# Moving half of an image's column layout from the prologue into layer 0, and reordering the passage to layer 1

## The chip, the cores and the metric

The kernel runs on one core of a Trainium2 chip. The metric is the device time of one execution in microseconds (us). Most executions of a kernel agree within 0.3%. The engines are PE (TensorE: matmuls and transposes), DVE (VectorE), ACT (ScalarE), POOL (GpSimd) and SP (SyncE, which issues most of the DMAs here). PE writes to PSUM, the others compute from SBUF or PSUM; 16 DMA engines move data between SBUF and the device's memory.

## The reference

The input x has shape (4, 16, 256, 256), float32: 4 images of 16 channels. Two layers follow, each with a residual:

```python
x = x + _L0_conv_ref(_gn(x), conv_w, conv_b)
x = x + _L1_conv_ref(_gn(x), base_weight, spline_weight, spline_scaler, bias_weight)
```

`_gn` normalises groups of two channels over the whole image (8 groups). Layer 0 is a 3x3 convolution from 16 to 400 channels, read as 25 logits for each of 16 channels at each pixel. A softmax over the 25 gives weights, and the output is the weighted sum of the pixel's 5x5 neighbourhood in the same channel:

```python
out = conv(x, conv_w, padding='SAME') + conv_b
weights = softmax(out.reshape(N, C, 25, H, W), axis=2)
return einsum('ncuij,ncuij->ncij', unfold5x5(x), weights)
```

Layer 1 takes each normalised pixel through SiLU and through 8 cubic B-spline basis functions; both sets of features go through a 3x3 convolution to 16 channels, and a bias is added.

## The kernel before, in words

**Layouts.** An image is handled in two halves `h` of 128 rows (rows are SBUF partitions), and a half in 8 strips of 32 columns: 64 strips in all, image by image, upper half first. Layer 0 reads three copies of the normalised image in device memory: `hs`, rows for the 5x5 neighbourhoods; `hst[b][h]`, the columns (transposed, 130 rows each: a half and one border row above and below); and `hsl[b][h]`, the same columns split into a rounded part `hi` and the remainder `lo`. `normalize(b, ...)` (line 264) makes these copies. It is a generator: each `next` does one step. For each quarter `q` of the channels, `rows(q)` has ACT normalise the x tile twice (lines 327 and 340: into the row layout `hsp`, and into `ht`). For `n` in 0, 1 and each half, `columns(q, n, h)` has PE transpose four pieces of `ht` into the PSUM tile `tp` (line 362), copies them to `tts[n]` and, rounded, `his[n]` (lines 355 to 359; the 128x4 copies are the border row that the other half needs), and subtracts on DVE to get `los[n]` (line 370). A list `moves` holds issues that fall due some steps later: row stores (line 288) after 4 steps, loads of the next x tile (line 280) after 4, ACT copies of the border into `los` (lines 312 and 313) after 5, and six column stores of 260 KB (line 302: three tiles, two halves) after 9. All these DMAs go to SP's queue.

**Prologue** (lines 399 to 589). It loads all four images for the statistics of the first normalisation (line 423 issues a load, DVE line 536, ACT's square line 543, PE line 546), prepares weights, and in between, with two steps per group of channels, runs `normalize(0, ...)` from tiles `held`. A check of the largest possible logit sets `flag`, which each engine reads at the branch (line 1110).

**Layer 0** (`layer0`, line 622). For each strip, 8 groups of 4 columns: PE makes the logits (lines 832 and 836) from the tiles `am` and `an` (lines 648 and 658, loaded two tiles of 8 columns ahead, 3 buffers), ACT takes the exponential (line 855) into `e` (4 buffers), POOL multiplies it by the neighbourhoods `u` (line 860; `u` loaded in line 672), and DVE reduces both over the 25 taps into `nd` (line 700), one group late. Each group ends with one `next` of the preparation of the following image, which so takes most of the 16 strips of an image; the last strip of an image finishes it. Some groups later the quotient of a strip is formed (DVE lines 720 to 722) and POOL subtracts it from `xc` (line 728). After four strips `xc` (1 MB) is stored to `x1s` (line 781), and its statistics for the second normalisation are taken. For the last strip these are DVE and POOL instructions (lines 759 to 773), and its store is issued by POOL. A written order (`in_order`, line 592) fixes the order on each engine as the program emits it.

**The passage and layer 1** (`layer1`, line 888). 64 units of 16 rows follow. For each, `load_x` (line 942) loads x into one of three tiles `xta`, `xtb`, `xtc`, 8 times over the partitions, 2 MB in two DMAs; `load_tiles` (line 957) loads 0.5 MB into one of three tiles `sl`, `slb` for the SiLU. ACT forms distances (line 990), and ACT and DVE the spline (lines 158 to 169) in two parts with the temporaries `ta` and `tb`, into the ring of rows `ring`. ACT applies the SiLU in `sl` (line 972), PE runs both convolutions (lines 1036 and 1046), DVE adds the bias (line 1019). The first instructions of layer 1 are placed before the last ones of layer 0, by marks that `layer0` returns. Tiles of layer 1 lie in the memory of layer 0's pools, one pool after the other, so that a tile can be written only when the tiles under it are done with. In order and in bytes per partition, layer 0 has `prep` (58880), `im` (24960), `l0` (two `u` of 11520, four `e` of 12800), `nd` (three of 4096) and `x1` (three `xc` of 8192, `z` 1024); layer 1 has `xta` (17408), `ta` and `tb` (three of 9216 each), `xtb` (17408), `pad` (1032), `ring` (51600), `sl` (8256), `xtc` (17408), `slb` (two of 8256) and the output tiles.

Of the kernel before, what the change touches and what calls it, by code (L numbers as in the profile page):

```python
# [11 lines left out]
F32 = mybir.dt.float32  # L12
F32R = mybir.dt.float32r
AF = mybir.ActivationFunctionType
# [20 lines left out]
def conv_preact_kernel(  # L35
# [12 lines left out]
    nc = tc.nc  # L48
# [3 lines left out]
    P = 128  # L52
# [208 lines left out]
                    hsl[b][h][:, :, w : w + RP].rearrange("c t r -> (c t) r"), zero[:, 0:RP],  # L261
                )

    def normalize(b, ptr, tiles, held=None, copier=None):

        prep, xps, tts, his, los = tiles
        copier = copier or nc.scalar.copy

        moves = [(20 + 4 * i, f) for i, f in enumerate(zeros(b, nc.sync))] if held is None else []

        def move():
            for f in [f for i, f in moves if i <= 0]:
# [18 lines left out]

        def put_columns(q, n):
            g0 = n * QG
            for h in range(NH):

                for to, ti, t in ((hst, 0, tts[n]), (hsl, 0, his[n]), (hsl, 1, los[n])):
                    d = to[b][h]
                    m = 2 if to is hsl else 1  # L300
                    t = t if t.dtype == F32 else t.bitcast(F32)
                    nc.sync.dma_start(
                        bass.AP(
                            tensor=d.tensor,
                            offset=d.offset + q * QC * m * CT + ti * CT + (1 + g0) * RP,
                            ap=[[QW * RP, W // QW], [m * CT, QC], [1, QG * RP]],
                        ),
                        t[:, h].rearrange("p g r -> p (g r)"),
                    )
# [5 lines left out]
        hts = {}  # L315

        def rows(q):
            for h in range(NH):
                xp = xps[h] if held is None else held[h][:, q * QC : (q + 1) * QC]
                hsp = prep.tile([P, NST, QC, SP], F32, name=f"hsp{b}_{q}_{h}", tag="hsp")  # L320
                ht = prep.tile([P, QW, W // QW, QC], F32, name=f"ht{b}_{q}_{h}", tag=f"ht{h}")
                hts[q, h] = ht
                for k in range(QC // GC):
                    g = q * (QC // GC) + k
                    kc = slice(k * GC, (k + 1) * GC)
                    how = dict(scale=nrm[b][:, 0, g : g + 1], bias=nrm[b][:, 1, g : g + 1])
                    nc.scalar.activation(
                        hsp[:, :, kc, :].rearrange("p s c w -> p c s w"),
                        bass.AP(
                            tensor=xp.tensor, offset=xp.offset + k * GC * (W + 2 * PAD),  # L330
                            ap=[xp.ap[0], [W + 2 * PAD, GC], [SW, NST], [1, SP]],
                        ),
                        AF.Identity, **how,
                    )
                    if k == QC // GC - 1:
                        nc.scalar.copy(hsp[:, 0, :, 0:PAD], zpad)
                        nc.scalar.copy(hsp[:, NST - 1, :, PAD + SW :], zpad)
                        moves.append((4, partial(put_rows, q, h, hsp)))
                    yield
                    nc.scalar.activation(  # L340
                        ht[:, :, :, kc].rearrange("p g w c -> p c w g"),
                        xp[:, kc, PAD : PAD + W].rearrange("p c (w g) -> p c w g", g=QW),
                        AF.Identity, **how,
                    )
                    if k == QC // GC - 1:
                        moves.append((4, partial(load, q + 1, h)))
                    yield

        def columns(q, n, h):

            tp = ptr.tile([P, QG, P], F32, name=f"tp{b}_{q}_{n}_{h}", tag="tp")

            def copy(t, to):

                to(t[:, h, :, 1 : 1 + P], tp)
                if h == 0:
                    to(t[:, 1, :, 0:1], tp[:, :, P - 1 :])
                else:
                    to(t[:, 0, :, RP - 1 :], tp[:, :, 0:1])

            for k in range(QG):
                nc.tensor.transpose(
                    tp[:, k, :], hts[q, h][:, n * QG + k].rearrange("p w c -> p (w c)"), ident
                )
            yield
            copy(tts[n], copier)
            copy(his[n], nc.scalar.copy)
            yield

            nc.vector.tensor_sub(  # L370
                los[n][:, h, :, 1 : 1 + P], tp, his[n][:, h, :, 1 : 1 + P].bitcast(F32)
            )
            if h == NH - 1:
                moves.append((5, partial(border, los[n])))
                moves.append((9, partial(put_columns, q, n)))
            yield
            yield
            yield
            yield

        for h in range(NH):
            load(0, h)
        yield
        for _ in rows(0):
# [2 lines left out]
        for q in range(C // QC):  # L387
            ahead = rows(q + 1) if q + 1 < C // QC else iter(())
            for n in range(QW // QG):
                for h in range(NH):  # L390
                    for k, _ in enumerate(columns(q, n, h)):
                        if k % 3 == 2:
                            next(ahead, None)
                        move()
                        yield
            for _ in ahead:
                move()
                yield
# [5 lines left out]
    with tc.tile_pool(name="prep0", bufs=2) as prep, tc.tile_pool(  # L404
# [121 lines left out]
        for b in range(B):  # L526
# [44 lines left out]
            if b == 1:  # L571
                prepare1()
            if b == 0:
                ahead = normalize(0, ptr0, tiles, held, nc.vector.tensor_copy)
                next(ahead)
        for _ in ahead:
            pass
# [42 lines left out]
    def layer0(shift):  # L620
# [4 lines left out]
        with tc.tile_pool(name=f"prep{arm}", bufs=2) as prep, tc.tile_pool(  # L625
# [62 lines left out]
            def after(k, f, *args):  # L688

                later.append([k, partial(f, *args)])  # L690
# [34 lines left out]
            def apply(n, nd, xc):  # L725
                w0 = strips[n][2] * SW % CX
                v = xc[:, :, w0 : w0 + SW]
                nc.gpsimd.tensor_sub(v, v, nd[:, 1])  # L728
                seeds[1:] = [newest(POOLE)]
                if w0 + SW == CX:  # L730
                    if n == len(strips) - 1:
                        after(1, last_statistics, n, xc)
                    else:
                        for g in range(G):
                            after(1 + g, statistics, n, xc, g)
                    after(2, store, n, xc)

            def columns_of(n):
                b, hf, s = strips[n]
# [57 lines left out]
            for n, (b, hf, s) in enumerate(strips):  # L797
                if (hf, s) == (0, 0):
                    for _ in ahead:
                        pass  # L800
                    ahead = normalize(b + 1, ptr, tiles) if b + 1 < B else iter(())
                    if b == B - 1:
                        bank = ptr.tile([P, QG, P], F32, name=f"ps{arm}", tag="tp")
                        first_scales = [scales(k, partial(lambda k: bank[:, k], k)) for k in range(2)]
                last = (hf, s) == (NH - 1, NST - 1)
                if last:
                    for _ in ahead:
                        pass
                u = us.pop(0)
                if s * SW % CX == 0:  # L810
# [3 lines left out]
                for j in range(0, SW, JG):  # L814
# [51 lines left out]
                    if len(waiting) > LAG:  # L866
                        sums()
                    step()
                    next(ahead, None)
                    if b == B - 1 and j % (SW // 2) == 0 and s > 0:  # L870
                        next(first_scales[j // (SW // 2)], None)
                if n == len(strips) - NST // 2:
# [12 lines left out]
    def layer1(arm, last, marks, seeds):  # L885
# [5 lines left out]
        with ExitStack() as pools:  # L891
# [1 line left out]
                return pools.enter_context(tc.tile_pool(name=f"{name}{arm}", bufs=bufs, **kw))  # L893


            def temps(name):
                p = pool(name)
                return [p.tile([P, RU // 2 + 1, W], F32, name=f"{name}{k}{arm}") for k in range(3)]

            def fixed(name, shape, n=1):  # L900
                p = pool(name)
# [1 line left out]
                return t  # L903

            XT = [P, RU + 1, W]
            xt0, tmp0, tmp1 = fixed("xta", XT), temps("ta"), temps("tb")
            xt1, pad = fixed("xtb", XT), fixed("pad", [P, W + 2])[0]
            ring = fixed("ring", [P, 3 * RU + 2, W + 2])[0]
            SL = [P, RU // RT, W + 2]
            sl = fixed("sl", SL)  # L910
            xtt = xt0 + xt1 + fixed("xtc", XT)
            sl += fixed("slb", SL, 2)
            yop = pool("yo", 3)
            pstat = pool("pstat1", space=PSUM)
            py = pool("py", 4, space=PSUM)
# [144 lines left out]
            load_tiles(0)  # L1060
            for half in range(2):
                load_x(1, half)
            nc.gpsimd.tensor_copy(pad, edge[:, 4:5].to_broadcast([P, W + 2]))
            for e in (0, W + 1):
                nc.gpsimd.tensor_copy(
# [6 lines left out]

            halo(0)
            set_up = newest(POOLE).name
            sides(sl[0])
            features(0, put)
            first_silu = len(nc.cur_bb.bb.instructions)
            silu(0)
            for n in range(len(units)):
                if n % 2:  # L1080
                    next(more, None)
                if n > 0:
                    features(n, put)
                    silu(n)
                    halo(n)
                if n + 2 < len(units):
                    for half in range(2):
                        load_x(n + 2, half)
                store()
                if n + 1 < len(units):  # L1090
                    load_tiles(n + 1)
                outputs(n)
                if n == 0:
                    for t in sl[1:]:
                        sides(t)
            for _ in range(LAG1):
                put(1)
                store(1)
# [61 lines left out]
```

## Time and profile before

| | us |
|---|---|
| median of 3 runs | 3076.96 |
| lowest and highest | 3075.38, 3077.81 |
| the profiled execution's own time | 3072.98 |
| its span | 3070.8 |
| busy in the span: DVE | 2959.4 |
| PE | 2807.1 |
| ACT | 2238.8 |
| POOL | 1954.8 |

The span reaches from the first to the last instruction of the profiled execution; the execution's own time has some 2 us around it. An engine's busy time is the sum of what its instructions took, without register and DMA-issuing ones. A line such as L700 is line 700 of the kernel. In a row of a view, `out<-in` names the written and the read tiles, `x512` is the number of instructions, and what stands in brackets, or after the bar, is the idle time before them and what ended it. SPq is SP's queue, in which DMAs are issued. The DMA share is the mean busy share of 16 DMA engines; it can go a little above 1.

### The profile page before, as it was taken

To read this page: it belongs to the slowest core of one execution; us is meant where nothing else is said; L and a number is where in the kernel's file an instruction comes from. 1 tells how busy PE (TensorE), PEld (TensorE's weight loads), DVE (VectorE), ACT (ScalarE), POOL (GpSimd) and SP (SyncE) were. 2 spreads that over 40 slices of the span, in tenths; PEclk is the share of its full clock that TensorE was granted. 3 is DMA by queue.
4 is the path that set the end of the run, shared out by engine and by line. 5 is a ranking of instruction groups with operands and counts; after the bars stand their busy time and mean duration, and the time that the engine had idled before them with its cause. 6 is when DMAs were issued, how large, how long until landed. Compare 5 with 4: busy or idle time off the path is not lost.

```text
span 3070.8 us, 39744 instructions
## 1 busy us (share of the span) xinstructions
PE 2807.1 (91%) x14248; PEld 1450.3 (47%) x14248; DVE 2959.4 (96%) x1587; ACT 2238.8 (73%) x2587; POOL 1954.8 (64%) x744
## 2 busy tenths in 40 slices
PE   4599999999999999999999999957999999999998
PEld 3366656656566656666666656531222222222222
DVE  7599999999999999999999999997999999999997
ACT  6466675576765666765645646667999999999996
POOL 4299999999999999999999999971100100000000
PEclk7699999999999999999999999978999999999999
DMA  8988977879888778878867657659999999999994
GB/s 272 297 222 224 247 218 197 232 184 256 225 218 233 201 206 238 234 209 226 224 162 189 184 149 199 175 118 179 193 193 196 199 195 188 198 197 201 189 199 90
DMA packets 350929, 626.29 MB, mean 204 GB/s; under 512 B 41330, under 2 KB 216676, under 8 KB 334852
## 3 DMA queue, kind: packets, MB, share of 16 engines
q1 hardware_dynamic: 318020, 605.29, 80.6%
q10 hardware_dynamic: 30960, 15.73, 1.8%
q0 software_dynamic: 1744, 2.64, 0.3%
q8 instruction: 117, 1.92, 0.3%
q14 instruction: 88, 0.72, 0.1%
HBM read 513.95 MB, written 104.24 MB: 201 GB/s over the span
## 4 chain that ended last, share of the span: by engine, by line
DVE 69%; issue 11%; PE 7%; DMA 6%; ACT 3%; POOL 2%; SPq 2%; DVEq 0%; ACTq 0%; POOLq 0%
DVE nd L700 44%; PE lg L832 4%; DVE ta L168 4%; DVE ta L167 4%; DVE tb L168 4%; DVE tb L167 4%; DVE tb L158 2%; POOL e L860 1%; DVE yo L1019 1%; DVE r L721 1%; PE lg L836 1%; DVE nd L720 1%; DMA xta<-x1s 1%; DVE nd L722 1%; DMA an<-hsl 1%
## 5 line engine op out<-in xcount | busy, mean ns | idle before, releaser
L860 POOL TENSOR_TENSOR e<-e,u 128x1600 f32<-128x1600 f32 x512 | 1789.4, 3552 | 48.4 <-ACT e L855 30.5
L832 PE MATMUL lg<-wm,am 128*128 128x400 f32 x4096 | 1737.1, 505 | 82.6 <-ACT e L855 47.3
L700 DVE TENSOR_REDUCE nd<-e 128x128 f32<-128x3200 f32 x512 | 1748.0, 3478 | 28.3 <-POOL e L860 28.1
L836 PE MATMUL lg<-wn,an 97*128 97x400 f32 x2048 | 1345.8, 657 | 15.3 <-DMA an<-hsl 15.2
L855 ACT ACTIVATE e<-lg 128x800 f32<-128x800 f32 x1024 | 820.5, 838 | 709.6 <-DVE nd L700 472.3
L832 PEld LDWEIGHTS lg<-wm,am 128*128 128x128 f32 x4096 | 761.8, 192 | 402.3 <-ACT e L855 96.4
L1036 PE MATMUL yp<-ring,wt 128*32 128x512 f32 x6144 | 748.7, 600 | 97.0 <-DVE ring L169 73.1
L836 PEld LDWEIGHTS lg<-wn,an 97*128 97x128 f32 x2048 | 388.3, 190 | 333.9 <-issue 23.1
L1036 PEld LDWEIGHTS yp<-ring,wt 128*32 128x32 f32 x6144 | 205.4, 109 | 632.3 <-issue 428.9
L953 POOL MEMSET sl<- 16x256 f32 x4 | 1.2, 306 | 307.6 <-PE yp L1046 301.4
L953 POOL MEMSET slb<- 16x256 f32 x4 | 1.2, 307 | 299.8 <-PE yp L1046 299.7
L168 DVE TENSOR_TENSOR ta<-ta,ta 128x2048 f32<-128x2048 f32 (+1 forms) x64 | 147.4, 2304 | 3.4 <-ACT ta L166 3.3
L169 DVE SCALAR_TENSOR_TENSOR ring<-ta,ta 128x2048 f32<-128x2048 f32 (+1 forms) x64 | 147.8, 2310 | 2.5
L747 ACT ACTIVATE z<-xc,nrm 128x256 f32<-128x256 f32 x240 | 144.2, 601 | 5.4 <-POOL xc L728 1.3
L169 DVE SCALAR_TENSOR_TENSOR ring<-tb,tb 128x2048 f32<-128x2048 f32 x64 | 145.6, 2275 | 2.5
L168 DVE TENSOR_TENSOR tb<-tb,tb 128x2048 f32<-128x2048 f32 x64 | 145.3, 2270 | 0.0
L1046 PE MATMUL yp<-slb,ws 64*32 64x512 f32 (+1 forms) x1008 | 128.2, 602 | 0.0
L166 ACT ACTIVATE ta<-ta 128x2048 f32<-128x2048 f32 (+1 forms) x64 | 123.4, 1928 | 2.0
L193 POOL TENSOR_TENSOR d<-d,nrz 128x8 f32<-128x8 f32 x4 | 2.7, 666 | 188.1 <-DVE d L191 188.1
L166 ACT ACTIVATE tb<-tb 128x2048 f32<-128x2048 f32 x64 | 120.5, 1883 | 0.0
L972 ACT ACTIVATE slb<-slb,q 64x2048 f32<-64x2048 f32 x42 | 87.9, 2094 | 21.5 <-DMA slb<-x1s 20.4
L728 POOL TENSOR_TENSOR xc<-xc,nd 128x512 f32<-128x512 f32 x64 | 83.3, 1302 | 8.3 <-DVE nd L722 8.3
(195 smaller groups left out, 2099.3 us busy)
## 6 DMA issues: line engine op xcount, KB each, us to landing
am<-hst SPq DMA_DIRECT2D x512, 194.6 KB
u<-hs SPq DMA_DIRECT2D x320, 288.0 KB
an<-hsl SPq DMA_DIRECT2D x512, 129.8 KB
xta<-x1s SPq DMA_DIRECT2D x40, 1024.0 KB
xtb<-x1s SPq DMA_DIRECT2D x40, 1024.0 KB
xtc<-x1s SPq DMA_DIRECT2D x40, 1024.0 KB
am<-hst SPq DMA_DIRECT2D x256, 129.8 KB
slb<-x1s SPq DMA_DIRECT2D x164, 128.0 KB
```

Source lines behind the costliest of these rows:

```text
L166: nc.scalar.activation(s1, r1, AF.Square, scale=2.0)
L167: nc.vector.scalar_tensor_tensor(s2, t, 2.0, s2, ALU.subtract, ALU.mult)
L168: nc.vector.tensor_mul(s1, s1, r1)
L169: nc.vector.scalar_tensor_tensor(f, s2, 0.0, s1, ALU.min, ALU.subtract if given else ALU.add)
L700: nc.vector.tensor_reduce(nd[:, :, :, j : j + JG].rearrange("p t c j -> p t j c"), e.rearrange("p t j m c d -> p t j c m d"), AX.XY, ALU.add,)
L747: nc.scalar.activation(z, v, f, scale=nrm[b][:, 0, g : g + 1], bias=nrm[b][:, 1, g : g + 1], accum_out=st1[b][:, t, g, columns_of(n) : col ...
L832: nc.tensor.matmul(lg[:, i, :NL], lhsT=am[:, o : o + P], rhs=wm.rearrange("p m c d -> p (m c d)"), start=True, stop=False,)
L836: nc.tensor.matmul(lg[:, i, :NL], lhsT=an[:, o : o + P], rhs=wn.rearrange("p m c d -> p (m c d)"), start=False, stop=True,)
L855: nc.scalar.activation(ev, lg[:, :, :NL], AF.Exp)
L860: nc.gpsimd.tensor_tensor(e[:, 1].rearrange("p j m c d -> p j (m c) d"), e[:, 0].rearrange("p j m c d -> p j (m c) d"), uv, ALU.mult,)
L1036: nc.tensor.matmul(yp[t * M : (t + 1) * M], lhsT=wt[:, d, e].rearrange("p r o -> p (r o)"), rhs=ring[:, r0 + t * RT + d : r0 + t * RT + d ...
L1046: nc.tensor.matmul(yp[t * M : (t + 1) * M], lhsT=ws[v, e].rearrange("p r o -> p (r o)"), rhs=sl[n % 3][v, t : t + NT + 1 : NT, e : e + W], ...
```

## The change

It has two parts.

*The first image's lower columns.* `normalize` gets an argument `part`. In the prologue it runs with `part=0`: rows are made as before, both halves are normalised and transposed, but columns are copied, subtracted and stored for the upper half alone. Of the lower half only the border row is taken, and the upper half's last row is kept in three small tiles `kept`. In layer 0 a second generator `late` runs with `part=1`: it loads the lower half of image 0 again, normalises it into `ht`, transposes it and makes and stores the lower half's columns, with the kept border. In these two a column store falls due after 4 steps rather than 9, and there are no border moves; a load falls due at once. During image 0 each group takes two steps rather than one: in strips 0 to 4 of `late`, from strip 5 on of the preparation of image 1, which started in strip 0 before. What is left of `late` is finished at strip 5; strip 8 is the first that needs its columns.

*The passage.* The last strip's store is emitted right behind its subtraction rather than two groups later behind the statistics. The `tb` temporaries have 8 rows rather than 9. `sl` has two tiles, in the place before `xtc`, and the third (`slc`) lies behind it. The tiles of unit 1 are loaded before the loop, between `load_x` of unit 1 and that of unit 2, rather than after the latter.

```diff
-    def normalize(b, ptr, tiles, held=None, copier=None):
+    NQ = QW // QG
+    kept = [
+        const.tile([P, C // QC * NQ, QG, 1], d, name=f"kept{i}") for i, d in enumerate((F32, F32R, F32R))
+    ]
+
+    def normalize(b, ptr, tiles, held=None, copier=None, part=None):
...
+        moves = moves if held is None and part is None else []
+        parts = range(NH) if part is None else (part,)
+        read = range(NH) if part != 1 else (1,)
...
         def put_columns(q, n):
             g0 = n * QG
-            for h in range(NH):
+            for h in parts:
...
         def rows(q):
-            for h in range(NH):
+            for h in read:
...
                     if k == QC // GC - 1:
-                        moves.append((4, partial(load, q + 1, h)))
+                        moves.append((4 if part is None else 0, partial(load, q + 1, h)))
...
-            def copy(t, to):
-
-                to(t[:, h, :, 1 : 1 + P], tp)
-                if h == 0:
-                    to(t[:, 1, :, 0:1], tp[:, :, P - 1 :])
+            def copy(t, to, keep):
+
+                if h in parts:
+                    to(t[:, h, :, 1 : 1 + P], tp)
+                if part == 1:
+                    to(t[:, 1, :, 0:1], keep[:, q * NQ + n])
+                elif h == 1:
+                    to(t[:, 0, :, RP - 1 :], tp[:, :, 0:1])
                 else:
-                    to(t[:, 0, :, RP - 1 :], tp[:, :, 0:1])
+                    to(t[:, 1, :, 0:1] if part is None else keep[:, q * NQ + n], tp[:, :, P - 1 :])
...
+            v = slice(1, 1 + P) if h in parts else slice(RP - 1, RP)
+            to = h if h in parts else 0
             nc.vector.tensor_sub(
-                los[n][:, h, :, 1 : 1 + P], tp, his[n][:, h, :, 1 : 1 + P].bitcast(F32)
+                los[n][:, to, :, v], tp[:, :, 0 : v.stop - v.start],
+                his[n][:, to, :, v].bitcast(F32),
             )
+            if part == 0 and h == 0:
+                moves.append((1, partial(
+                    nc.scalar.copy, kept[2][:, q * NQ + n], los[n][:, 0, :, P : P + 1]
+                )))
+            if part == 1:
+                nc.scalar.copy(los[n][:, 1, :, 0:1], kept[2][:, q * NQ + n])
             if h == NH - 1:
-                moves.append((5, partial(border, los[n])))
-                moves.append((9, partial(put_columns, q, n)))
+                if part is None:
+                    moves.append((5, partial(border, los[n])))
+                moves.append((9 if part is None else 4, partial(put_columns, q, n)))
...
-                ahead = normalize(0, ptr0, tiles, held, nc.vector.tensor_copy)
+                ahead = normalize(0, ptr0, tiles, held, nc.vector.tensor_copy, 0)
...
                     if n == len(strips) - 1:
+                        store(n, xc)
                         after(1, last_statistics, n, xc)
                     else:
                         for g in range(G):
                             after(1 + g, statistics, n, xc, g)
-                    after(2, store, n, xc)
+                        after(2, store, n, xc)
...
+                    if b == 0:
+                        late = normalize(0, ptr, tiles, part=1)
...
+                if n == NST // 2 + 1:
+                    for _ in late:
+                        pass
...
-                    next(ahead, None)
+
+                    for _ in range(2 if b == 0 else 1):
+                        next(late if n <= NST // 2 else ahead, None)
...
-            xt0, tmp0, tmp1 = fixed("xta", XT), temps("ta"), temps("tb")
+            xt0, tmp0, tmp1 = fixed("xta", XT), temps("ta", RU // 2 + 1), temps("tb", RU // 2)
...
-            sl = fixed("sl", SL)
+            sl = fixed("sl", SL, 2)
             xtt = xt0 + xt1 + fixed("xtc", XT)
-            sl += fixed("slb", SL, 2)
+            sl += fixed("slc", SL)
...
             for half in range(2):
                 load_x(1, half)
+            load_tiles(1)
...
-                if n + 1 < len(units):
+                if 0 < n < len(units) - 1:
                     load_tiles(n + 1)
```

## The prediction

> **What bounds the kernel now.** I read the page, then cut the span at four events and asked for busy times by stage. Columns: PE, PEld, DVE, ACT and POOL busy, PE clock, DMA share, GB/s.
>
> ```profile
> 0.00:119.28 119.28, 49.92 (x216) 41.61 (x216) 86.95 (x268) 78.06 (x116) 36.73 (x90) 0.66 0.95 300
> 119.28:158.78 39.50, 27.66 (x78) 17.33 (x78) 13.96 (x5) 14.00 (x19) 18.21 (x22) 0.76 0.92 241
> 158.78:2046.10 1887.32, 1793.05 (x6269) 1154.92 (x6267) 1880.22 (x766) 1188.86 (x2006) 1849.95 (x580) 0.99 0.78 207
> 2046.10:2098.99 52.89, 34.71 (x240) 7.84 (x240) 34.34 (x35) 23.54 (x14) 22.98 (x22) 0.74 0.73 154
> 2098.99:3070.80 971.81, 901.80 (x7448) 228.59 (x7448) 943.96 (x517) 934.35 (x435) 26.89 (x31) 0.98 0.92 187
> ```
>
> Five regimes. In the prologue no engine is full, but DMA is (1.04 to 1.07 from 80 us on). The start of layer 0 has holes. Layer 0 is DVE-bound, 1880 of 1887 us. The passage has DVE idle for 18.5 of 53 us. Layer 1 has DVE, ACT and DMA all near full.
>
> The timelines of the two ends of the prologue's load queue, of layer 0's start, and of the passage:
>
> ```profile
> 64.51 0.89 SPq L423 DMA_DIRECT2D xin<-in_x_dram  x1
> 84.33 0.62 SPq L423 DMA_DIRECT2D xin<-in_x_dram  x1
> ...
> 144.40 0.87 ACT L327 ACTIVATE hsp<-xp,nrm 128x576 f32<-128x576 f32 x1 [7.93 <-DMA xp<-in_x_dram]
> 146.79 3.51 POOL L860 TENSOR_TENSOR e<-e,u 128x1600 f32<-128x1600 f32 x1 [6.66 <-ACT e L855]
> ...
> 2079.96 1.28 POOL L781 DMA_DIRECT2D x1s<-xc  x1
> 2086.19 0.22 POOL L1071 MEMSET slb<- 128x8 f32 x4 [4.95 <-DMA x1s<-xc]
> ```
>
> The last two image loads leave SP's queue only at 64.51 and 84.33, behind the stores of the columns. In the passage, the last strip's store starts at 2079.96 behind POOL's statistics; slb lies in that strip's memory, so unit 1's tiles are loaded only at 2086.19. Who waited there:
>
> ```profile
> ACT slb L972 <- DMA slb<-x1s: 20.4, 2, 18.6
> DVE tb L158 <- ACT xtc L990: 16.7, 1, 16.7
> ```
>
> DVE stands still from 2082.25 to 2098.99. Last, DVE's groups in layer 0:
>
> ```profile
> L370 DVE TENSOR_TENSOR lo<-tp,hi 128x512 fp32r<-128x512 f32 x48 | 32.7, 681 | 0.0
> ```
>
> **What the Trainium skill says.** Its page "DMA: Bandwidth & Descriptors", section Issuing engines are not separate DMA queues, says that all issued DMAs run on the same 16 engines and interleave. The trace agrees: SP waited 12.5 us in one place while ACT's x1s store was under way. So moved traffic meets layer 0's own. The Trainium skill's "TensorE: Matmul & The Clock Gate", section The HAM clock gate, says that an idle window of about 3.4 us halves the clock. The trace agrees in kind: after 2.49 us idle at 430 us a pair of L832 takes 1.54 instead of 0.83 us. The Trainium skill's "Perfetto Trace Analysis", section Identifying Performance Opportunities, asks to look for the bound by regime, since it changes over time; the windows above do.
>
> **The change part by part** (a group is four columns of a strip, a step one resumption of the preparation), against the profiled execution: 3072.98 us, that is the span of 3070.8 and 2.2 around it. The median of the runs, 3076.96, is 3.98 us higher.
>
> *Prologue, -10.5.* For the lower half of image 0 it still normalises and transposes everything and keeps one border column. Per (q, n), eight times, it drops from DVE a copy (0.67) and most of a subtraction (0.68, leaving some 0.15 each), from ACT a cast (0.6) and two border casts (0.2 each) less one kept copy (0.2), and from SP three stores of 260 KB. Sums: DVE 8 x 1.2 = 9.6, ACT 8 x 0.8 = 6.4, SP 24 issues x 0.6 = 14.4 us, 6.4 MB (19 us at the 338 GB/s of 80 to 100 us). These can't all count. Following SP: before the load at 64.51 there were six column stores and two row stores, 58.81 to 64.51. Now a column store is due after four steps, not nine, so (0,0)'s three go in SP's idle time at 45 to 58, and (0,1)'s three remain: about 3 us earlier. Between there and 84.33 twelve stores shrink to three (9 x 0.6 = 5.4 us), and the rows that they wait for come 2 to 3 us earlier from ACT: the last load leaves about 11 us earlier. Then ACT's order takes over: from its square at 75.15 to that of the last half at 94.21 its work shrinks by about 2 us and its waits for DVE and the load by 4, so I expect the last square 6 us earlier. From it to the flag (97.83 to 112.70) is a chain that stays, less some 0.7. From the flag to the branch (112.70 to 119.28) there was a tail of columns waiting for store buffers, and SP's last stores; half is gone, 4 us. Sum 6 + 0.7 + 4 = 10.7, taken as 10.5. Bounds: 5 (only the tail), 15 (also the load's whole 11).
>
> *Start of layer 0, +2.8.* Two steps are taken per four columns, so ACT meets the first `ht` one block of exponentials earlier. Before, ACT waited at xp's landing with two POOL blocks in hand (133.13 to 140.14). Now it has one. One load of 512 KB instead of two lands some 2.4 us earlier (0.5 MB at about 220 GB/s): about 142, counted from the old branch. `ht` (1.3) and two exponentials (0.84 each) follow; POOL's second block starts at 145, the third at 148.5. The second xp load waits on SP for `ht` and lands near 151.5, so the fourth block starts at 154.5 and the fifth at 158 where it was 155.21. Bounds 0 and +6.
>
> *Lower columns in layer 0, +5.4.* Eight subtractions of 681 ns on the engine that is full, 5.45 us; no cover. The ACT work (16 `ht` of 1.32, 16 copies of 0.6, small ones of 0.2: 36 us over 27 steps) lies under ACT's 700 us of idle time; the 32 transposes under PE's lead.
>
> *Doubled rate in image 0, +3.* Before, preparing image 1 moved 21.7 MB in 114 steps (427 us): 51 GB/s on about 174 (image 3, mostly 156 and 191). Now the late columns move 8.5 MB in 27 groups (100 us), and image 1 follows in 57 groups (217 us): 174 + 100 = 274 GB/s, DMA share about 1.0. The highest 30 us stretch of layer 0 shows 282 GB/s at 1.06 with DVE full. And tp has one buffer: transposes now come every 3 groups (11.8 us), while the trace has 12 to 20 us between a transpose and its subtraction, two groups apart; with one group, 8 to 16. PE's lead is clipped to about 11.8; POOL's product needs it 8.7 before, so about 3 us of cover stays. Between 0 and +15; I take 3.
>
> *Passage, -13.* The store is issued right after the subtraction, at 2063.9, and lands by 2070.1 (6.2 us as before). Unit 1's tiles go to a second sl buffer in e's memory and load at 2049, so the SiLU runs at 2074.5. What is late next is unit 2's x. By the sizes, xtc moves from 151000-168408 to 156184-173592 bytes past layer 0's first pool (a second sl of 8256, three tb rows of 1024 less), and the last xc begins at 170368. So its load waits for the store: from 2063.87 to 2070.1. With some 11 us for 2 MB (xtb: 13.2 behind 0.5 MB of tiles) it lands at 2081.2 and ACT's L990 starts there, not at 2095.15: 13.9. DMA then has 3 MB a unit at 195 to 200 GB/s for 15.25 us, so I take 0.9 back. Bounds: 16.7 (DVE's hole) and 9.
>
> *At nothing.* Smaller tb, kept tiles (384 bytes), ACT's copies of kept columns: 8 x 3 x 0.2 us under ACT's idle time. The POOL statistics are 1.3 us later; nothing near reads them.
>
> Sum: -10.5 + 2.8 + 5.4 + 3 - 13 = -12.3. 3072.98 - 12.3 = 3060.7; on the median 3064.7.
>
> **Rivals.** (1) *The prologue doesn't shorten by more than its tail*, because ACT's order or the statistics decide: -5 + 2.8 + 5.4 + 5 - 13 = -5, 3072. For it: ACT is busy 18.3 of 20 us from 60 to 80. Against: SP's queue and DMA are full from 80 on. (2) *Slower: DMA becomes the bound in strips 5 to 12.* 59.5 MB in 217 us need 274 GB/s. If that mix gets only 230, they take 259: 42 us more. Some 17 us are covered (prefetch and POOL's lead), 25 stay in place of my 3: +10, 3087. It is slower than before by 0.2% from 21 us of stall, 232 GB/s or so. For it: layer 1 gets only 200 at share 1. Against: 282 seen in this stage. (3) *Everything pays*: prologue 15, passage 15, stalls 1: -21, 3056. (4) The move changes nothing, the passage waiting elsewhere: I give it no share of its own, since the releasing store is in the trace.
>
> **From cases to numbers.** Mine 0.66 (3056 to 3071), rival (1) 0.17, (2) 0.12, (3) 0.05. What counts as no change is 0.2%, 6.2 us. Mine and (3) are faster, a quarter of (1) too, the rest of it the same; (2) is slower: 0.75, 0.13, 0.12. Range 3050 to 3077: it leaves out (2), some of (1) and the far end of (3).
>
> **What would show it.** The branch near 109 instead of 119.28; the last xin issue near 73; POOL's fifth block 2 to 4 us later after the branch; 56 L370 in layer 0; DVE idle in strips 0 to 12 of a few us; x1s<-xc issued on POOL right after L728; L990 of xtc 12 to 14 us earlier against the last L700. Wrong if DVE waits for POOL in strips 5 to 12 by tens of us, or the branch comes after 115.

## The result

The changed kernel takes 3068.05 us (median of 12 runs, 3062.36 to 3079.5) against 3076.07 us of the kernel before (12 runs, 3073.17 to 3093.56): a ratio of 0.9972, interval 0.9956 to 0.9989, or 8.0 us less. A second set, on the chip of the last runs below (22 and 36 runs), gave 0.9976, interval 0.9966 to 0.9986. The prediction was 3064.7 in a range of 3050 to 3077.

The profiled execution of the changed kernel, at 3079.5 us, happens to be the slowest of its set. Cut at the same events as the kernel before, the first cut being the branch to within some 0.2 us (columns: stretch, its length, busy PE, PEld, DVE, ACT, POOL, PE clock, DMA share, GB/s):

```profile
0.00:108.50 108.50, 47.98 (x216) 40.92 (x216) 74.90 (x257) 70.78 (x99) 36.76 (x90) 0.76 0.89 275
108.50:155.60 47.10, 26.80 (x86) 17.39 (x86) 17.50 (x9) 17.08 (x23) 18.17 (x22) 0.73 0.73 187
155.60:2055.46 1899.86, 1799.34 (x6293) 1157.81 (x6291) 1884.40 (x774) 1205.38 (x2051) 1849.98 (x580) 0.99 0.77 210
2055.46:2095.74 40.28, 22.15 (x138) 4.93 (x142) 34.34 (x34) 23.52 (x13) 17.20 (x22) 0.67 0.89 192
2095.74:3077.50 981.76, 912.89 (x7554) 233.73 (x7546) 945.57 (x517) 934.43 (x435) 31.63 (x31) 0.99 0.93 185
```

The prologue is 10.8 us shorter and the passage 12.6; the start of layer 0 is 7.6 longer and its body 12.5. The last stretch, layer 1, is 10 us longer, although its instructions are the same. That is not the change: in a second profile of the same kernel that stretch takes 970.5 us, and over the profiles below it lies at 970 to 973, at 976 to 977, or at 981 to 982, whichever kernel it is. So I compare stage by stage, and read the stages up to layer 1.

The table has the first profile of before and both of after. The start is counted from the issue of the first `am` load, some 1.1 to 1.3 us behind the branch.

| us | before | after | after, second | predicted difference |
|---|---|---|---|---|
| first `am` issue | 120.60 | 109.72 | 108.98 | -10.5 |
| from there to POOL's fifth block | 34.6 | 42.4 | 41.9 | +2.8 |
| from there to the end of the last reduction | 1890.9 | 1903.4 | 1903.8 | +8.4 |
| from there to DVE's first work on unit 2 | 52.9 | 40.3 | 40.0 | -13 |
| from there to the end | 971.8 | 981.8 | 970.5 | 0 |
| span | 3070.8 | 3077.5 | 3065.1 | -12.3 |

Now the lines that answer to those shown of before. The two last image loads, in SP's queue, and the casts that write the flag, in the kernel before (L589) and after (L616):

```profile
64.27 0.87 SPq L450 DMA_DIRECT2D xin<-in_x_dram  x1
77.20 0.70 SPq L450 DMA_DIRECT2D xin<-in_x_dram  x1
```

```profile
112.56 0.14 DVE L589 CAST flag<-bd 1x1 int32<-1x1 f32 x1
108.47 0.14 DVE L616 CAST flag<-bd 1x1 int32<-1x1 f32 x1
```

The first load leaves where it did (64.51 before), the second 7.1 us earlier (84.33). The flag is written 4.1 us earlier, and the first `am` goes out 1.1 us behind it where it took 7.9. The start of layer 0, in the timelines of SP's queue, ACT, PE and POOL:

```profile
128.00 10.68 SPq L292 DMA_DIRECT2D xp<-in_x_dram  x2
134.43 1.27 ACT L354 ACTIVATE ht<-xp,nrm 128x512 f32<-128x512 f32 x1 [11.71 <-DMA xp<-in_x_dram]
137.16 3.52 POOL L893 TENSOR_TENSOR e<-e,u 128x1600 f32<-128x1600 f32 x1 [10.72 <-ACT e L888]
138.31 1.12 PE L379 MATMUL tp<-ident,ht 128*128 128x128 f32 x4 [13.05 <-ACT ht L354]
142.11 0.84 ACT L888 ACTIVATE e<-lg 128x800 f32<-128x800 f32 x1 [3.85 <-PE lg L869]
144.75 3.54 POOL L893 TENSOR_TENSOR e<-e,u 128x1600 f32<-128x1600 f32 x1 [4.07 <-ACT e L888]
```

This is a chain of waits. ACT stands 11.71 us for `xp`; then PE, which has stood 13.05 us behind four transposes for `ht`, begins the logits that come after them; and POOL's third block, predicted right behind the second, waits 4.07 us for those. In the kernel before PE had no transposes there and ran on while ACT waited, until the logits' buffers were full. The second `xp` load stands in SP's queue until 138.7 and the next `am` behind it; but between 138 and 156 us PE waits for neither `am` nor `an`, so that costs nothing there.

The passage, and who waited in it:

```profile
2073.52 1.26 POOL L809 DMA_DIRECT2D x1s<-xc  x1 [0.30 <-POOL xc L755]
2078.92 1.16 SPq L977 DMA_DIRECT2D xtc<-x1s  x2
2091.91 3.80 ACT L1025 ACTIVATE xtc<-xtc,q 128x4096 f32<-128x4096 f32 x1 [5.03 <-DMA xtc<-x1s]
2095.74 1.23 DVE L158 TENSOR_SCALAR tb<-xtc 128x2048 f32<-128x2048 f32 x1 [3.21 <-ACT xtc L1025]
```

```profile
ACT xtc L1025 <- DMA xtc<-x1s: 5.0, 1, 5.0
DVE tb L158 <- ACT xtc L1025: 3.2, 1, 3.2
```

The store goes out right behind POOL's subtraction, and 5.4 us later the load of `xtc` can start; the SiLU's 18.6 us of waiting for `slb` are gone, and DVE's hole of 16.7 us is 3.2. Last, the subtractions of the columns in layer 0, and the waits around them between 165 and 1050 us (waiter, releaser: us in total, times, longest):

```profile
L389 DVE TENSOR_TENSOR lo<-tp,hi 128x512 fp32r<-128x512 f32 x56 | 38.1, 681 | 1.6 <-ACT hi L370 1.6
```

```profile
PEld tp L379 <- DVE lo L389: 16.1, 13, 3.8
PE tp L379 <- DVE lo L389: 10.8, 7, 3.3
DVE nd L727 <- POOL e L893: 10.1, 7, 4.5
```

The kernel before, in the same window:

```profile
DVE nd L700 <- POOL e L860: 1.1, 1, 1.1
```

There are 56 subtractions for 48, as predicted. New are waits of PE for the subtraction, and 10.1 us in which DVE waits for POOL, where it was 1.1. One of them, in strip 5:

```profile
309.16 0.68 DVE L389 TENSOR_TENSOR lo<-tp,hi 128x512 fp32r<-128x512 f32 x1
309.90 1.12 PE L379 MATMUL tp<-ident,ht 128*128 128x128 f32 x4 [3.35 <-DVE lo L389]
310.81 1.54 PE L865 MATMUL lg<-wm,am 128*128 128x400 f32 x2
314.39 0.84 ACT L888 ACTIVATE e<-lg 128x800 f32<-128x800 f32 x1 [3.86 <-PE lg L869]
317.56 3.51 POOL L893 TENSOR_TENSOR e<-e,u 128x1600 f32<-128x1600 f32 x1 [5.22 <-ACT e L888]
321.11 3.49 DVE L727 TENSOR_REDUCE nd<-e 128x128 f32<-128x3200 f32 x1 [0.48 <-POOL e L893]
```

PE stands 3.35 us until the one `tp` is free, comes back at half speed (1.54 us for a pair that takes 0.84), and the lack passes through ACT and POOL to DVE.

### The profile page after: what moved, and what is told of

It reads as the page before. It is cut to its first block, busy times and chain, and to the rows that moved or that the text cites. A ratio compares the mean times of both kernels' runs of the same rounds, so it can differ in the third digit from the quotient of the medians.

```text
span 3077.5 us, 39857 instructions
## 1 busy us (share of the span) xinstructions
PE 2809.2 (91%) x14280; PEld 1454.8 (47%) x14280; DVE 2956.7 (96%) x1587; ACT 2251.2 (73%) x2619; POOL 1953.7 (63%) x744
## 4 chain that ended last, share of the span: by engine, by line
DVE 68%; issue 11%; PE 7%; DMA 5%; ACT 4%; POOL 2%; SPq 2%; DVEq 0%; POOLq 0%; ACTq 0%
DVE nd L727 45%; PE lg L865 4%; DVE ta L168 4%; DVE ta L167 3%; DVE tb L168 3%; DVE tb L167 3%; POOL e L893 2%; DVE tb L158 2%; DMA sl<-x1s 2%; DVE yo L1054 1%; PE lg L869 1%; DVE r L748 1%; DVE nd L747 1%; DVE nd L749 1%; DVE lo L389 1%
## 5 line engine op out<-in xcount | busy, mean ns | idle before, releaser
L893 POOL TENSOR_TENSOR e<-e,u 128x1600 f32<-128x1600 f32 x512 | 1789.5, 3555 | 71.2 <-ACT e L888 64.7
L168 DVE TENSOR_TENSOR ta<-ta,ta 128x2048 f32<-128x2048 f32 (+1 forms) x64 | 147.6, 2306 | 11.9 <-ACT ta L166 11.9
L1081 PE MATMUL yp<-sl,ws 64*32 64x512 f32 (+1 forms) x1032 | 131.2, 602 | 0.0
L1007 ACT ACTIVATE sl<-sl,q 64x2048 f32<-64x2048 f32 x43 | 90.0, 2094 | 13.5 <-DMA sl<-x1s 12.6
```

Source lines behind the costliest of these rows:

```text
L168: nc.vector.tensor_mul(s1, s1, r1)
L893: nc.gpsimd.tensor_tensor(e[:, 1].rearrange("p j m c d -> p j (m c) d"), e[:, 0].rearrange("p j m c d -> p j (m c) d"), uv, ALU.mult,)
L1081: nc.tensor.matmul(yp[t * M : (t + 1) * M], lhsT=ws[v, e].rearrange("p r o -> p (r o)"), rhs=sl[n % 3][v, t : t + NT + 1 : NT, e : e + W], ...
```

## The experiments

Four theories are put to the test. *Passage*: the two parts of the change are independent, and the passage alone brings its 12 us. *A*: in layer 0 the single `tp` buffer clips PE's lead (how far its logits run ahead of POOL) at the doubled rate. *B*, its rival: the denser transfers make the holes. *S*: the start is late because ACT and PE stand in their queues behind an `ht` whose load is under way; its rivals are the number of steps taken there and the load's own traffic.

**Each part alone.** First the kernel before with the passage's part of the diff, then the changed kernel with that part undone:

```diff
                     if n == len(strips) - 1:
+                        store(n, xc)
                         after(1, last_statistics, n, xc)
...
-            sl = fixed("sl", SL)
+            sl = fixed("sl", SL, 2)
...
+            load_tiles(1)
```

> The kernel before with the passage's half of the change alone (store behind the subtraction, two tiles in sl, early tiles of unit 1, tb of 8 rows). My theory: the passage's gain stands by itself. The traces of before and after show 52.9 and 40.3 us from the last L700 of layer 0 to the first spline instruction of unit 2, so 12 to 13 us faster than before, and layer 1 after that as long as before. Rival (what the passage gains is given back to DMA in layer 1, which is near full): 5 us or less.

> The change without its passage: only the lower columns are moved. My theory from the two traces: the branch 10.8 us earlier, the start of layer 0 7.7 us longer, eight subtractions of 0.68 (5.4), and holes on DVE in strips 5 to 12 of 5 to 9 us; so 7 to 12 us slower than before by the one profiled execution, 4 to 5 slower by the medians (8 us gained in all, 12.6 of them in the passage). Rival: the prologue's gain is what the change lives on, and this alone is 3 us or more faster than before.

The passage alone: 3063.24 us, ratio 0.9964, interval 0.9951 to 0.9977, 11.9 us less than before, and no slower than the whole change. Its profile shows the store and the new, shorter hole:

```profile
2064.62 1.26 POOL L782 DMA_DIRECT2D x1s<-xc  x1 [0.30 <-POOL xc L728]
2088.27 1.23 DVE L158 TENSOR_SCALAR tb<-xtc 128x2048 f32<-128x2048 f32 x1 [4.86 <-ACT xtc L991]
```

The columns alone: 3085.21 us, ratio 1.0042, interval 1.0027 to 1.0056: slower than before, by 10 us between the medians and some 13 by the ratio, in six runs. Its profile, the fastest of them at 3074.85, has the early `am` issue (108.22), the late fifth block (42.0 us on) and DVE's hole before `xtc` (14.96 us). From `am`'s issue to the end of the last reduction it takes 1941.2 us, 15.7 more than before, against 12.4 gained in the prologue: a loss of 3.3 us. The two profiles of the whole change have 20.2 and 20.1 there against 10.9 and 11.6, a loss of 9.3 and 8.5. So all of the gain is the passage's; the columns' part loses more in layer 0 than it gains ahead of it. How much it loses varies with the execution; what made the other five runs of the columns alone longer than the profiled one, no profile shows.

**The subtraction's source.** To free `tp` early, `lo` was made from the copy `tt` in SBUF:

```diff
-                los[n][:, to, :, v], tp[:, :, 0 : v.stop - v.start],
+                los[n][:, to, :, v], tts[n][:, to, :, v],
```

> The changed kernel, but the subtraction for lo reads the copy tts in SBUF and not tp in PSUM, so that tp is free once ACT has copied it and DVE no longer holds it. Theory A (PE's transposes wait for the one tp buffer, PE's lead is clipped and its clock halves): the 27 us in which PE waits for L389 before a transpose vanish, DVE's holes in strips 5 to 12 shrink from about 10 us to 3 or less, 5 to 9 us faster than the change. Theory B (the holes come from am and an arriving late while DMA is near full): within 2 us of the change, holes as before.

A miss: 3168.35 us, ratio 1.0298, interval 1.0284 to 1.0312. The subtraction itself grew. Over the whole kernel, and one place in layer 0:

```profile
L389 DVE TENSOR_TENSOR lo<-tt,hi 128x512 fp32r<-128x512 f32 x64 | 149.8, 2341 | 4.9 <-ACT hi L370 4.9
```

```profile
422.23 10.49 POOL L893 TENSOR_TENSOR e<-e,u 128x1600 f32<-128x1600 f32 x3 [1.45 <-ACT e L888]
429.24 4.03 DVE L389 TENSOR_TENSOR lo<-tt,hi 128x512 fp32r<-128x512 f32 x1
```

It takes 2341 ns on average instead of 681, and here it is over at 433.27, 0.55 us behind the end of POOL's third product (432.72), beside whose whole length it ran. That is the rule here: of the 56 in layer 0, 52 end 0.2 to 0.7 us behind the end of one of POOL's products. The Trainium skill's page "SBUF — State Buffer", section SBUF: two separate sides, says that a DVE operation with two SBUF inputs and a GpSimd operation that reads SBUF share one pair of ports under an exclusive lock, held for a whole instruction, so that the later one blocks. The traces agree: in the changed kernel the operation with one input in PSUM takes 681 ns beside the same products. This run says nothing on A.

**The start, with fewer steps.** One step per group in the first two groups of strip 0:

```diff
-                    for _ in range(2 if b == 0 else 1):
+                    for _ in range(2 if b == 0 and (n > 0 or j > JG) else 1):
```

> The changed kernel with one step rather than two in the first two groups of layer 0. Theory: the longer start (43.6 us from the branch to POOL's fifth block, 35.9 before) comes from the normalisation and the transposes standing in ACT's and PE's queues before the first x tile has landed; with one step POOL has two blocks in hand again and the start is 36 to 38 us, so 6 to 8 us faster than the change. Rival (the start is longer because DMA delivers am, an, u and xp later): the start stays at 42 or more, within 2 us of the change.

3067.45 us, ratio 0.9973, interval 0.9962 to 0.9985: no different from the change. POOL has its second block in hand again (two in a row at 120.83), but the fifth starts 41.1 us after `am`'s issue. The block that the prediction counted as lost was not what made the start late.

**A: the subtraction in the step of its transposes.** For `late` and image 1, with the source in PSUM as it was, the two pauses in between go behind it:

```diff
+            soon = part == 1 or b == 1
+            if not soon:
-            yield
+                yield
             copy(tts[n], copier, kept[0])
             copy(his[n], nc.scalar.copy, kept[1])
-            yield
+            if not soon:
+                yield
...
+            if soon:
+                yield
+                yield
```

> The change, but for image 0's lower half and image 1 a column's copies and its subtraction are emitted in the same step as its four transposes (the freed steps follow at the end), so tp comes free one group earlier and PE may lead by three groups instead of two. Theory A (the single tp buffer clips PE's lead at the doubled rate, and that is most of layer 0's loss beyond the eight subtractions): PE's waits for the subtraction fall from 27 us to under 8, DVE's waits for POOL in strips 0 to 12 from some 10 us to under 4, and the kernel is 4 to 7 us faster than the change, ratio to the kernel before about 0.995. Theory B (the denser transfers make the holes): PE's waits for the subtraction fall, but the holes and the time stay, ratio 0.997.

3063.26 us, ratio 0.9951, interval 0.9935 to 0.9967: by the ratios some 6 to 8 us less than the change, as A says, though the intervals overlap; the stage has to decide. The waits in the same window, 165 to 1050 us:

```profile
PEld tp L379 <- DVE lo L392: 4.0, 4, 1.6
PE tp L379 <- DVE lo L392: 2.2, 3, 1.1
```

and DVE waits for POOL 2.0 us instead of 10.1. The steps' pace and what they transfer are unchanged.

**Image 1 at three steps per two groups.** This gives `tp` more time and thins the traffic too:

```diff
-                    for _ in range(2 if b == 0 else 1):
+                    for _ in range(2 - j // JG % 2 * (n > NST // 2) if b == 0 else 1):
```

> The change, but image 1 is prepared at three steps per two groups instead of four, in strips 5 to 14. If the doubled rate of image 1 costs by its traffic or by tp (rival 2 of the prediction in small), the stretch from strip 5 on loses its holes, 2 to 4 us faster than the change, ratio 0.9962. If the loss is in strips 0 to 4, nothing changes: 0.9972.

3064.67 us, ratio 0.9955, interval 0.9938 to 0.9971. The time alone does not tell it from the change, but the stage does. From 302 to 510 us, roughly strips 5 to 12, the window of the kernel before:

```profile
302.00:510.00 208.00, 199.02 (x704) 127.81 (x702) 207.52 (x87) 138.43 (x252) 201.62 (x63) 0.99 0.85 232
```

The same window of the change, in its second profile:

```profile
302.00:510.00 208.00, 192.47 (x675) 124.02 (x674) 198.18 (x90) 149.33 (x285) 186.88 (x58) 0.96 0.91 255
```

Of the subtraction in the step of its transposes:

```profile
302.00:510.00 208.00, 199.03 (x712) 127.72 (x710) 205.50 (x92) 153.75 (x292) 195.75 (x61) 0.98 0.96 261
```

And of image 1 at three steps per two groups:

```profile
302.00:510.00 208.00, 198.15 (x715) 127.56 (x714) 207.52 (x90) 154.67 (x287) 201.96 (x63) 1.00 0.92 255
```

And of the kernel with both mends, which comes last below:

```profile
302.00:510.00 208.00, 199.03 (x721) 128.52 (x720) 207.59 (x89) 150.36 (x284) 199.58 (x62) 1.00 0.97 266
```

What to read is DVE's busy time, the third in each row: 207.5 of 208 us before, 198.2 with the change, and back at 205.5 when `tp` comes free earlier, with *more* bytes per second than the change (261 against 255). So 7.3 of the 9.3 us are `tp`'s, with both mends all of them, and B falls for this stage. Three steps in two groups get the same back at the change's own 255 GB/s. The size of the loss varies with the execution: DVE is busy for 197.5 us in the first profile of the change, and for 202.2 to 202.9 in the four profiles of other kernels here that leave `tp` and the pace as the change has them, so 5 to 10 us are lost; no profile with `tp` freed earlier, or with the slower pace, shows less than 205.5.

**S: the lower columns from strip 1, and the load alone in strip 0.** One kernel prepares nothing in strip 0; the other issues the first load there as the change does, but lets 14 steps pass before the first `ht`:

```diff
-                        next(late if n <= NST // 2 else ahead, None)
+                        if b > 0 or n > 0:
+                            next(late if n <= NST // 2 else ahead, None)
```

```diff
         for h in read:
             load(0, h)
         yield
+        for _ in range(14 if part == 1 else 0):
+            yield
```

> The change, but nothing is prepared in strip 0; the lower columns begin in strip 1. Theory S (at the start the first transposes stand in PE's queue ahead of later logits and wait for ht, which waits for xp's load): POOL's fifth block starts 36 us or less after the branch (35.9 before, 43.6 with the change), and the kernel is about 7 us faster than the change, ratio to the kernel before about 0.995. Rival: the start is late because am's own loads come late from columns just stored; then the fifth block stays at 41 us or more after the branch and the ratio at 0.997.

> The change, but between the first load of xp and the first ht of the lower columns the preparation lets 14 steps pass, so that the load still goes out in the first group while ht and the transposes come at the end of strip 0. If the start is late because ACT and PE stand in their queues behind an ht whose load is under way (theory S), POOL's fifth block starts some 27 us after am's first issue, as with the columns begun in strip 1 (26.5; the change: 42.4), and the kernel is 4 to 8 us faster than the change. If the load's own traffic is what delays the first blocks, the fifth stays above 36.

From strip 1: 3059.88 us, ratio 0.9947, interval 0.9931 to 0.9963. With the load first: 3054.74 us, ratio 0.9939, interval 0.9922 to 0.9955, 10 us less than the change by the ratios, 12 between the medians on its chip, and more than expected. POOL's first blocks in the latter's timeline:

```profile
120.78 31.36 POOL L895 TENSOR_TENSOR e<-e,u 128x1600 f32<-128x1600 f32 x9 [11.93 <-DMA an<-hsl]
```

And the load of `xp` in SP's queue:

```profile
124.31 0.40 SPq L292 DMA_DIRECT2D xp<-in_x_dram  x1
```

In both, nine blocks run without a gap, and the fifth starts 26.5 us after `am`'s issue instead of 42. In the second the load goes out early all the same and disturbs none of these blocks; what cost was standing behind it. Neither its traffic nor the number of steps made the start late. Of the 15.5 us about 9 last with the columns from strip 1, where the thirteenth block starts at 62.1 against 71.1 and 70.5, and 12 with the load first (58.7): the first `ht` and transposes, now at the turn of strip 0, cost a short wait of their own.

**The mends together, and without the passage.** The first has the subtraction in its step and the columns from strip 1; the second adds three steps per two groups; the third is the first with the passage's part undone. Their diffs are those above.

> The subtraction in the step of its transposes and the lower columns begun in strip 1, together. If theories A and S both hold, their gains add up: 11 to 14 us faster than the change, ratio to the kernel before about 0.993, and faster than the kernel with the passage alone (0.9964). If only one holds, 0.995; if the columns' loss is in the DMA traffic, 0.997.

> Both mends (the subtraction in the step of its transposes, the lower columns from strip 1) and image 1 at three steps per two groups. With tp free early the denser traffic should be all that is left: if it costs nothing (theory A alone), the time is that of both mends, 0.993 of the kernel before; if it still costs, 1 to 3 us less.

> The columns' part alone with both mends, without the passage. The columns alone were at 1.0042. If the two mends bring what they bring in the whole change, about 12 us, the columns' part is at 0.998 to 1.000: paid back, with little gained; if parts and mends are independent of the passage, it is 11 to 12 us above both mends with the passage, 0.997.

> The change itself, unaltered, on the chip of these runs: 0.997 of the kernel before, PE's waits for the subtraction near 27 us, the fifth block some 42 us after am's first issue, and layer 1 at 971 us from unit 2's distance on, not the 982 of the profile first taken, if those 11 us are a variation between executions.

Both mends: 3056.58 us, ratio 0.9931, interval 0.9914 to 0.9947, clear of both intervals of the change and of that of the passage alone, and 21 us below the kernel before. The two gains add up to within the noise. With the slower pace 3055.41, ratio 0.9936, interval 0.9918 to 0.9954, 19 us below: nothing more, so the density that is left costs nothing that can be seen. With the load first alone, without the mend of A, the chip of the slower pace gave 3054.74, which the intervals do not tell from these two; DVE is busy for only 202.8 us from 302 to 510 there, so something is left to gain, but the load first together with the mend of A was not run. The columns with both mends, but without the passage: 3067.79, ratio 0.9981, interval 0.9968 to 0.9993; the columns' part now pays by some 6 us where it cost 10. From `am`'s issue to the end of the last reduction the profiles show 1925.5 us before, 1945.7 with the change, 1927.1 with both mends: 1.6 above before, though 5.4 us of subtraction have been added to DVE.

The changed kernel on the chip of these last runs: 3066.59, ratio 0.9976; its start and waits are as in its first profile, and layer 1 takes 970.5 us. The 11 us of the first profile are thus a variation between executions. In that execution the stretch from 2500 to 2700 us shows a DMA share of 1.01 and 185 GB/s, in the second 0.93 and 193; why, no run here shows. Differences of that size between the spans of single profiles therefore say nothing by themselves.

## Why the prediction was right, and where its steps were not

*Prologue, -10.5: right as a sum, wrong in its terms.* It measured -10.9 to -12.4 over the profiles, by the first `am` issue. The last `xin` load left at 77.20, not near 73: it gained 7.1 us of the 11 counted. The last square on ACT started at 90.97 and 90.29 in the two profiles of the change, where it was at 94.21: 3.2 and 3.9 us earlier, not 6. From there to the flag the chain became 0.9 us shorter, about the 0.7 said. What made up for it is the tail. From the flag to the first `am` it had taken 7.9 us and now takes 1.1, a gain of 6.8 where "half is gone, 4 us" was counted: all of it went. That two errors of 2 to 3 us cancelled is luck.

*Start of layer 0, +2.8: wrong, +7.2 to +7.8, beyond its upper bound of +6.* The failing step is "`ht` (1.3) and two exponentials (0.84 each) follow; POOL's second block starts at 145, the third at 148.5". Counted from the first `am`, `ht` was to start at 21.4 us; it did at 24.7 and 23.8 in the two profiles, no sooner than `xp` was used before (23.8). The load left SP's queue 0.9 to 2.0 us later than before and took 6.4 to 6.6 us from issue to use, where two had taken 7.5: not 2.4 us less. And the third block's logits were not ready: the transposes stood before them in PE's queue, which cost POOL another 4.1 to 4.4 us. That the fourth block did not wait for the second load gave some 2 us back. The prediction costed ACT's and SP's queues for the moved step and left PE's out.

*Lower columns, +5.4: right* in number and duration, 56 subtractions of 681 ns.

*Doubled rate, +3: right in its mechanism, for the change too small.* Layer 0's body grew by 12.5 to 12.9 us in the two profiles of the change, so 7.1 to 7.5 are left for it, within 0 to 15; with the columns alone, which have the same body, it grew by 8.3 in the one profile, which leaves 2.9. The term that was mis-sized is the cover: "so about 3 us of cover stays". In the place shown in strip 5 none is left: the three operations of the strip's division (0.67, 0.69 and 0.69 us) stand ahead of the subtraction in DVE's queue, and PE comes back from its wait at half speed. Of the two reasons given, it was `tp`, not DMA: the run with more traffic lost less.

*Passage, -13: right*, -12.6 and -12.9 in the profiles, 11.9 us by the medians of the passage alone. What is late next is unit 2's `x`, as said.

*The sum* was to be -12.3 and is -5.7 between the profiles with like layer 1, -8.0 between the medians; the first gap is the two terms of layer 0, 4.4 us at the start and 4.5 at the doubled rate, less what the prologue (1.1) and layer 1 (1.3) gave beyond theirs. The prediction's own four terms of the columns' part come to +0.7 us, so it too gave the whole gain to the passage, without saying so; measured they are +9.3, +8.5 and, with the columns alone, +3.3. *The rivals:* (1), only the tail, falls: the flag too came 4.1 us earlier, and the branch at 108.5; but the tail was the larger half of the gain. (2), DMA as the bound in strips 5 to 12, falls with the runs for A; its place was right and its cause wrong. (3), everything pays, falls with both terms of layer 0. (4) falls with the passage alone. *One reading:* the 12.5 us that SP waited, given there as agreement on transfers that interleave, is the wait of an issue queue, put down to the end of that store; it does not show two transfers sharing the engines, and no term rests on it.

## What to carry to other kernels

When work is moved into the start of a pipelined loop, follow it through every in-order queue that it enters: here a step that waited for a load held back all that stood behind it on ACT and PE, and fourteen steps of delay between issuing the load and using it were worth some 10 us. When the pace of a helper is doubled, its single buffers are what to look at first, and how soon the reader that frees them is emitted; here moving two pauses behind the subtraction got back what looked like bandwidth. And parts of a change should be timed apart: here one part carried the whole gain and hid that the other lost.

## What the runs showed of the hardware

A DVE subtraction of 128x512 fp32 with one input in PSUM takes 681 ns beside POOL's products, and with both inputs in SBUF 2341 ns on average, ending in 52 of 56 cases 0.2 to 0.7 us behind a product of POOL; in that run POOL's products took 3569 ns on average, 3555 in the changed kernel. A pair of PE's logit matmuls took 1.54 us instead of 0.84 right behind a wait of 3.35 us. Thirteen profiles of kernels with the same instructions in layer 1 showed it at 970 to 973, 976 to 977 or 981 to 982 us, a spread as large as the effects studied here.
